# Page loads and fused-pass loads issued by ScalarE, layer-0 fillers by SyncE, in a two-layer GNN and mixture-of-experts kernel

## The chip, the cores and the metric

The kernel runs on one core of one Trainium2 chip. Times are device microseconds (us) of one execution. An execution that the profiler recorded has a span, from the first recorded instruction to the last, and its own time, which is a little longer.

The engines are named as the profile names them: PE (matrix unit; PEld is its weight load), DVE (vector), ACT (scalar), POOL (GpSimd), SP (sync; it has no arithmetic and here only issues DMAs). SPq and ACTq in the profile are instructions of the two engines that only the sequencer executes: DMA issues, register moves, semaphore waits.

## The reference

Two layers over 8192 tokens (128 graphs of 64 nodes) of 256 channels. Each layer is a graph network and then a mixture of experts; both add to the residual.

```python
# layer 0
x = x + gnn0(layernorm(x), adj)          # adj @ x, 256 -> 1024, RMS norm, silu, 1024 -> 256
n = layernorm(x)
logits = einsum('bsd,ed->bse', n, gate_w)                      # 64 experts
top_logits, indices = top_k(logits, 6)
scores = softmax(top_logits)
xW = einsum('bsd,bskde->bske', n, lattice_weights[indices])    # 256 x 256 per expert
lattice_out = einsum('bske,bsk->bse', xW, scores)
proj = einsum('bsd,ed->bse', lattice_out, out_w) + out_b
x = x + layernorm(n + proj) * ln_g + ln_b
# layer 1
n = layernorm(x);  h = layernorm(n) * gamma + beta
x = x + n + relu((adj @ h) @ W_rel + b_rel + h @ W_root)
n = layernorm(x)
x = x + sum over the top 2 of 8 experts of n: w * (relu(n @ W1[e] + b1[e]) @ W2[e] + b2[e])
```

## The kernel before

Four stages follow one another on the core.

**Stage 0, layer 0's graph network (to about 770 us).** It works through 32 blocks of 256 tokens, chooses six experts for each token, and scatters each token's row six times into a table in HBM, `r0x`, so that the rows of one expert lie together (line 277, indirect DMAs of POOL). A row carries its 256 values, the place where its answer belongs, and its weight. A page table is then computed: a page is 128 rows of one expert, and for each page it holds the row where the page starts and the expert.

**Stage 1, the pages of layer 0 (785 to 1476 us).** 447 pages are handled as 224 pairs. Three functions are staggered: at step s the kernel calls `fetch(s + 12)`, `flip(s + 3)` and `apply(s)`.

- `fetch` reads the start rows of four pages from the page table into registers (`Router.load`, line 372, once every second pair) and loads each page of the pair from HBM to a tile `px0` or `px1` (line 378, 129 KB each; 16 buffers of each name).
- `flip` transposes the pair on PE (line 736) into PSUM (`pt`, 4 buffers), and ACT copies it to SBUF (line 738, `pxT`, 5 buffers).
- `apply` multiplies the pair with its experts' matrices on PE (line 751, into `py`, 4 buffers in PSUM), scales each row by its weight on DVE (line 756, `py_s`, 8 buffers), and sends each page's 128 answers to `r0y` in HBM by an indirect DMA of POOL (line 284, `reply`). For the first 64 pairs it also calls `fill_end` (line 361), which stores a page of filler rows behind the rows of one expert in the table (line 157, 129 KB each), so that the last page of an expert that is not full reads defined rows. Full pages come first in the page table and are loaded without waiting for the fillers.

**Stage 2, the fused pass (1476 to 1903 us).** 32 blocks again. For a block, `load3` loads its six answers a token (`y`, 1536 KB, line 793, 2 buffers), the normed input `xn1` and the residual `x1` (lines 795 and 797, 256 KB each, 3 buffers), and two halves of the adjacency (line 473). `mixture` adds the six answers by transposing matmuls (line 807), ACT copies the sum to `accT` (line 810), and `out_proj` multiplies it with `out_w` on PE (line 818). Then come the layer norm, the graph network of layer 1, the choice of two experts and the scatter to `r1x`. The functions are staggered by block: at one step `load3(s + 2)` is called first, `mixture(s + 1)` and `out_proj(s + 1)` after it. `load_w2`, once in each of eight steps, loads one of the eight matrices `fw2` that the last stage needs (512 KB).

**Stage 3, layer 1's experts (1903 to 2449 us).** Pages of 256 rows, their weights loaded by SP, two matmuls, answers added to `out_x` by POOL.

The order of the instructions on PE, DVE and ACT is the one in which the program calls them (`tc.manual_schedule`). The order on SP and POOL is the scheduler's. DMAs of SP and ACT, in the scheduler's order over both, take turns on eight semaphores ("lanes"): each waits until the DMA eight before it has landed.

Before the change SP issues all loads of stages 1 and 2, and ACT issues the fillers:

```python
staggered(npair, ((-12, fetch), (-3, flip), (0, apply)))      # stage 1
staggered(NB, ((-2, load3), (0, layer_out_h), (3, choose1), (-1, mixture), ...))   # stage 2
```

Of the kernel before, what the change touches and what calls it, by code (L numbers as in the profile page):

```python
# [13 lines left out]
ENG = mybir.EngineType  # L14
# [5 lines left out]
P = 128  # L20
# [50 lines left out]
class Router:  # L71
# [286 lines left out]
        v.scalar_tensor_tensor(exp, ispart, -float(E), kind, op0=ALU.mult, op1=ALU.add)  # L358
        v.tensor_scalar(self.tab[:, 1, :], exp, float(E - 1), None, op0=ALU.min)

    def fill_end(self, e):

        if e % 4 == 0:
            _, self.ends = self.nc.values_load_multi_w_load_instructions(
                self.last[0:1, e:e + 4], engines=[ENG.Activation], min_val=0, max_val=self.spare - self.pg,
                skip_runtime_bounds_check_because="the rows of an expert end in its chunk")
        self.fill(self.nc.scalar, self.ends[e % 4])

    def load(self, what, i, engine):

# [3 lines left out]
            skip_runtime_bounds_check_because="the page table holds no other values for any counts")  # L374
        return v

    def fetch(self, i, row, out):
        d = self.nc.sync.dma_start(out=out, in_=self.table[ds(row, self.pg), :].rearrange("(t p) d -> p t d", p=P))  # L378
        if i < self.full_pages:
            self.tc.declare_no_dep(d.ins, group=self.name + "fill", reason="full pages have no filler rows")  # L380
            self.tc.add_to_no_dep_group(self.name + "full", d.ins)
# [11 lines left out]
def two_layer_gnn_moe_kernel(ctx: ExitStack, tc: tile.TileContext, a: dict, out: bass.AP):  # L393
# [8 lines left out]
    C = T * P  # L402
# [57 lines left out]
    def by_tile(ap):  # L460
        return ap.rearrange("(t p) d -> p t d", p=P)
# [5 lines left out]
        nc.gpsimd.memset(at, 0.0)  # L467
        adjacency.append(at)

    def load_adjacency(b):  # L470
        at = adjacency[b % 4]
        for g in range(2):
            nc.sync.dma_start(out=at[g * G:(g + 1) * G, :, g * G:(g + 1) * G],
                              in_=adjT[2 * b * T + g:2 * (b + 1) * T:2].rearrange("t m n -> m t n"))
        return at

# [25 lines left out]
    with tc.tile_pool(name="c0", bufs=1) as c0, \  # L502
# [15 lines left out]
        def load0(b):  # L518
            B = blocks[b]
            B["x"] = x = x_view[:, b % 4 * T:(b % 4 + 1) * T, :]  # L520
            nc.sync.dma_start(out=x, in_=by_tile(x_in[ts(b, C), :]))
            B["at"] = load_adjacency(b)

        load0(0)
        load0(1)
# [187 lines left out]
    with tc.tile_pool(name="wx0", bufs=3) as wx, \  # L713
            tc.tile_pool(name="pt1", bufs=4, space=PSUM) as pt_pool, \
            tc.tile_pool(name="py1", bufs=4, space=PSUM) as py_pool:
        npair = (r0.pages + 1) // 2
        pairs = [dict() for _ in range(npair)]
        regs = {}

        def fetch(j):  # L720
            Q = pairs[j]
            for q in range(2):
                i = 2 * j + q
                if i % 4 == 0:
                    regs["row"] = r0.load(0, i, ENG.SP)
                if i < r0.pages:
                    Q["px", q] = px = wx.tile([P, 1, W], F32, name=f"px{q}", bufs=16)
                    r0.fetch(i, regs["row"][i % 4], px)

        def flip(j):  # L730
            Q = pairs[j]
            pt = pt_pool.tile([P, KD, C], F32, name="pt")
            n = min(2, r0.pages - 2 * j)
            for q in range(n):
                for k in range(KD):
                    nc.tensor.transpose(pt[:, k, ts(q, P)], Q["px", q][:, 0, ts(k, P)], ident)  # L736
            Q["xT"] = xT = wx.tile([P, KD, C], F32, name="pxT", bufs=5)
            nc.scalar.copy(xT[:, :, :n * P], pt[:, :, :n * P])  # L738

        def apply(j):  # L740
            Q = pairs[j]
            if j < E0:
                r0.fill_end(j)
            if j % 2 == 0:
                regs["e"] = r0.load(1, 2 * j, ENG.PE)
            py = py_pool.tile([P, 2, D], F32, name="py")
            y = wx.tile([P, 2, D], F32, name="py_s", bufs=8)
            n = min(2, r0.pages - 2 * j)
            for q in range(n):
                for k in range(KD):  # L750
                    nc.tensor.matmul(py[:, q, :], lhsT=Q["xT"][:, k, ts(q, P)],  # L751
                                     rhs=lat[:, ds(regs["e"][(2 * j + q) % 4], 1), k, :].rearrange("p o d -> p (o d)"),
                                     start=(k == 0), stop=(k == KD - 1))
            for q in range(n):
                px = Q["px", q]
                nc.vector.tensor_scalar(y[:, q, :], py[:, q, :], px[:, 0, D + 1:D + 2], None, op0=ALU.mult)  # L756
                r0.reply(px[:, 0, :], y[:, q, :])

        staggered(npair, ((-12, fetch), (-3, flip), (0, apply)))
    lat_pool.__exit__(None, None, None)  # L760


# [5 lines left out]
    with tc.tile_pool(name="c3", bufs=1) as c3, \  # L768
# [21 lines left out]
        def load3(b):  # L790
            B = blocks[b]
            B["y"] = y = work.tile([P, T, K0, D], F32, name="y")
            nc.sync.dma_start(out=y, in_=r0.answer[ts(b, C * K0), :].rearrange("(t p k) d -> p t k d", p=P, k=K0))
            B["xn1"] = xn1 = work.tile([P, T, D], F32, name="xn1", bufs=3)
            nc.sync.dma_start(out=xn1, in_=by_tile(xn1_dram[b]))
            B["x1"] = x1 = work.tile([P, T, D], F32, name="x1", bufs=3)
            nc.sync.dma_start(out=x1, in_=by_tile(x1_dram[b]))
            B["at"] = load_adjacency(b)

        def mixture(b):  # L800

# [168 lines left out]
    with tc.tile_pool(name="wx1", bufs=2) as wx, \  # L970
            tc.tile_pool(name="pt4", bufs=2, space=PSUM) as pt_pool, \
            tc.tile_pool(name="ph4", bufs=4, space=PSUM) as ph_pool, \
            tc.tile_pool(name="py4", bufs=2, space=PSUM) as py_pool:
        PG = 2 * P
        pages = [dict() for _ in range(r1.pages)]
        regs = {}

        def fetch1(i):
            Q = pages[i]
            if i % 4 == 0:  # L980
                regs["row"], regs["esp"] = r1.load(0, i, ENG.SP), r1.load(1, i, ENG.SP)
            row, e = regs["row"][i % 4], regs["esp"][i % 4]
            Q["x"] = x = wx.tile([P, 2, W], F32, name="px", bufs=4)
            r1.fetch(i, row, x)
            Q["w"] = w = wx.tile([P, F1W], F32, name="pw", bufs=3)
            nc.sync.dma_start(out=w, in_=fw1[ds(e, 1)].rearrange("o p f -> p (o f)"))  # L986
            Q["b2"] = b2 = wx.tile([P, D], F32, name="pb2", bufs=4)
            nc.sync.dma_start(out=b2, in_=a["L1_ffn_b2"][ds(e, 1), :].to_broadcast([P, D]))

        def flip1(i):  # L990
            Q = pages[i]
            pt = pt_pool.tile([P, KD, PG], F32, name="pt")
            ops.transpose(pt, Q["x"])
            Q["xT"] = xT = wx.tile([P, KD, PG], F32, name="pxT")
            nc.scalar.copy(xT, pt)

        def up(i):
            Q = pages[i]
            w = Q["w"]
            Q["hid"] = hid = wx.tile([P, KF, PG], F32, name="phid")  # L1000
            for c in range(KF):
                ph = ph_pool.tile([P, PG], F32, name="ph")
                for k in range(KD):
                    nc.tensor.matmul(ph, lhsT=w[:, k * F1 + c * P:k * F1 + (c + 1) * P], rhs=Q["xT"][:, k, :],  # L1004
                                     start=(k == 0), stop=(k == KD - 1))
                nc.scalar.activation(hid[:, c, :], ph, AF.Relu, bias=w[:, KD * F1 + c:KD * F1 + c + 1], scale=1.0)  # L1006

        def down(i):
            Q = pages[i]
            if i < E1:  # L1010
                r1.fill_end(i)
            if i % 4 == 0:
                regs["e"] = r1.load(1, i, ENG.PE)

            p = wx.tile([P, 2], F32, name="p")
            nc.scalar.activation(p, Q["x"][:, :, D + 1], AF.Exp)  # L1016
            nc.vector.tensor_scalar(p, p, 1.0, None, op0=ALU.add)  # L1017
            nc.vector.reciprocal(p, p)
            py = py_pool.tile([P, 2, D], F32, name="py")
            y = wx.tile([P, 2, D], F32, name="py_s")  # L1020
            for t in range(2):
                for c in range(KF):
                    nc.tensor.matmul(py[:, t, :], lhsT=Q["hid"][:, c, ts(t, P)],  # L1023
                                     rhs=fw2[:, ds(regs["e"][i % 4], 1), c, :].rearrange("p o d -> p (o d)"),
                                     start=(c == 0), stop=(c == KF - 1))
            nc.vector.tensor_add(y, py, Q["b2"].unsqueeze(1).to_broadcast([P, 2, D]))  # L1026
            for t in range(2):
                nc.vector.tensor_scalar(y[:, t, :], y[:, t, :], p[:, t:t + 1], None, op0=ALU.mult)
                r1.add(i, Q["x"][:, t, :], y[:, t, :])

        staggered(r1.pages, ((-2, fetch1), (0, flip1), (1, down), (0, up)))
# [32 lines left out]
```

## Time and profile before

| | |
|---|---|
| median of 14 runs | 2449.61 us (2442.52 to 2479.59) |
| profiled execution: its own time | 2451.15 us |
| profiled execution: its span | 2449.1 us |
| PE busy, share of the span | 2072.6 us, 85% |
| PEld | 1758.9 us, 72% |
| DVE | 1238.9 us, 51% |
| ACT | 1047.5 us, 43% |
| POOL | 1249.6 us, 51% |

The span in 40 equal slices of 61 us; each digit is the busy share of a slice in tenths, PEclk the granted clock of PE:

```
PE   3998888888862888888788877899997799999997
DVE  3778888888864222222222324788876222222221
ACT  2877767777751111211111113566554233333332
POOL 1165666666566666666666660333333344444344
PEclk9999999999985899989999999998998899999999
DMA  7133333333364777655555437878772676666665
```

Stage 0 is slices 1 to 13, stage 1 slices 13 to 24, stage 2 slices 25 to 31, stage 3 the rest. In the rows of the profile, L378 is line 378 of the kernel; a row of a group has the line, the engine, the operation, the tiles written and read, the count, the busy time and the mean of one in ns, the idle time of the engine ahead of them, and what ended most of that. In the table of waits a row names who waited for whom, the total in us, the times, and the longest.

HBM traffic over the span is 404 MB, 167 GB/s on average. SP issued 447 loads of px in stage 1 and 32 loads of each kind (64 adjacency halves) in stage 2; ACT issued the 64 fillers.

### The profile page before, as it was taken

How to read it: one execution, taken by the hardware profiler on the slowest of the kernel's cores; microseconds unless marked ns; L12 is line 12 of the kernel's file. 1: busy time of each engine (PE TensorE's matmuls, PEld its weight loads, DVE VectorE, ACT ScalarE, POOL GpSimd, SP SyncE). 2: the span in 40 equal slices, each digit the busy share in tenths (PEclk: the TensorE clock that was granted, in tenths of full speed). 3: DMA queues.
4: the chain of work that ended last, by engine and by line, in shares of the span. 5: the costliest groups of instructions: out<-in, count | busy, mean ns of one | idle time of the engine just before them, and what ended most of it. 6: DMA issues, size and time to landing. Idle time of an engine off the chain costs nothing. (4 is left out here: it accounts for less than half of the span.)

```text
span 2449.1 us, 38858 instructions
## 1 busy us (share of the span) xinstructions
PE 2072.6 (85%) x10870; PEld 1758.9 (72%) x10870; DVE 1238.9 (51%) x4053; ACT 1047.5 (43%) x2061; POOL 1249.6 (51%) x1238
## 2 busy tenths in 40 slices
PE   3998888888862888888788877899997799999997
PEld 3877777777751776766666666788776688888886
DVE  3778888888864222222222324788876222222221
ACT  2877767777751111211111113566554233333332
POOL 1165666666566666666666660333333344444344
PEclk9999999999985899989999998999998899999999
DMA  7133333333364777655555437878772676666665
GB/s 222 57 123 108 112 120 114 108 115 113 111 206 132 223 223 216 191 161 171 167 175 162 138 100 272 266 250 266 242 236 79 171 170 163 167 158 162 155 163 116
DMA packets 289696, 404.39 MB, mean 165 GB/s; under 512 B 57657, under 2 KB 243273, under 8 KB 289489
## 3 DMA queue, kind: packets, MB, share of 16 engines
q1 hardware_dynamic: 205168, 251.04, 34.4%
q0 software_dynamic: 66480, 136.68, 18.5%
q10 hardware_dynamic: 17840, 14.21, 1.8%
q8 instruction: 94, 1.54, 0.3%
q14 instruction: 114, 0.93, 0.1%
HBM read 228.78 MB, written 181.23 MB: 167 GB/s over the span
## 5 line engine op out<-in xcount | busy, mean ns | idle before, releaser
L284 POOL DMA_INDIRECT r0y<-py_s,px x447 | 439.1, 982 | 251.3 <-DVE py_s L756 127.2
L751 PE MATMUL py<-lat,pxT 128*128 x1788 | 470.6, 405 | 67.9 <-issue 52.4
L277 POOL DMA_INDIRECT r0x<-xs,r0row x384 | 411.2, 1071 | 202.7 <-issue 101.1
L756 DVE TENSOR_SCALAR py_s<-py,px 128x256 f32<-128x256 f32 x447 | 186.9, 478 | 506.7 <-PE py L751 181.3
L751 PEld LDWEIGHTS py<-lat,pxT 128*128 128x128 f32 x1788 | 343.4, 203 | 128.2 <-issue 70.4
L292 POOL DMA_INDIRECT out_x<-py_s,px x142 | 221.1, 1557 | 319.2 <-DMA out_x<-py_s,px 209.3
L738 ACT COPY pxT<-pt 128x512 f32<-128x512 f32 x224 | 125.7, 588 | 582.8 <-remote 173.2
L1006 ACT ACTIVATE phid<-ph,pw 128x256 f32<-128x256 f32 x284 | 134.7, 474 | 334.3 <-issue 210.7
L1004 PE MATMUL ph<-pxT,pw 128*128 128x256 f32 x1136 | 258.8, 381 | 2.4 <-DMA pw<-in_L_ffn_W1b 2.4
L1023 PE MATMUL py<-fw,phid 128*128 x1136 | 256.9, 379 | 0.0
L618 PE MATMUL ps<-lat 128*128 128x256 f32 x1024 | 254.0, 392 | 0.7 <-issue 0.7
L1004 PEld LDWEIGHTS ph<-pxT,pw 128*128 128x128 f32 x1136 | 217.2, 191 | 32.7 <-issue 2.8
L575 PE MATMUL ph<-lat 128*128 128x256 f32 x1024 | 232.7, 386 | 3.3 <-DVE lat L609 1.4
L1023 PEld LDWEIGHTS py<-fw,phid 128*128 128x128 f32 x1136 | 210.4, 190 | 25.7
L736 PE MATMUL pt<-ident,px 128*128 128x128 f32 x894 | 153.9, 290 | 83.0 <-DMA px<-r0x 69.9
L277 POOL DMA_INDIRECT r1x<-xs,r1row x128 | 127.7, 998 | 178.5 <-issue 83.9
L575 PEld LDWEIGHTS ph<-lat 128*128 128x128 f32 x1024 | 195.1, 193 | 30.5 <-DVE lat L609 2.1
L618 PEld LDWEIGHTS ps<-lat 128*128 128x128 f32 x1024 | 192.6, 195 | 26.2 <-issue 2.7
L736 PEld LDWEIGHTS pt<-ident,px 128*128 128x128 f32 x894 | 118.4, 150 | 126.5 <-issue 64.6
L578 ACT ACTIVATE lat<-ph,c_L_gnn_b 128x256 f32<-128x256 f32 x256 | 102.1, 469 | 112.0 <-PE ph L575 85.6
L1017 DVE TENSOR_SCALAR p<-p 128x2 f32<-128x2 f32 x71 | 13.6, 191 | 249.8 <-ACT p L1016 239.7
L1026 DVE TENSOR_TENSOR py_s<-py,pb 128x512 f32<-128x512 f32 x71 | 49.1, 692 | 159.0 <-PE py L1023 156.8
(259 smaller groups left out, 3004.2 us busy)
## 6 DMA issues: line engine op xcount, KB each, us to landing
px<-r0x SPq DMA_DIRECT2D x447, 129.0 KB
y<-r0y SPq DMA_DIRECT2D x32, 1536.0 KB
pw<-in_L_ffn_W1b SPq DMA_DIRECT2D x71, 514.0 KB
px<-r1x SPq DMA_DIRECT2D x71, 258.0 KB
x<-x SPq DMA_DIRECT2D x64, 256.0 KB
pb<-in_L_ffn_b SPq DMA_DIRECT2D x71, 128.0 KB
r0x<-r0filler ACTq DMA_DIRECT2D x64, 129.0 KB
lat<-in_x SPq DMA_DIRECT2D x32, 256.0 KB
```

The costliest lines, as they stand in the source:

```text
L277: i = self.nc.gpsimd.indirect_dma_start(out=self.table[:, :], out_offset=bass.IndirectOffsetOnAxis(ap=row[:, t, k:k + 1], axis=0), in_=xs[ ...
L284: i = self.nc.gpsimd.indirect_dma_start(out=self.answer[:, :], out_offset=bass.IndirectOffsetOnAxis(ap=x[:, self.D:self.D + 1].bitcast(I32 ...
L292: i, d = f"{self.name}add{i}", self.nc.gpsimd.indirect_dma_start(out=self.total[:, :], out_offset=bass.IndirectOffsetOnAxis(ap=x[:, self.D ...
L575: nc.tensor.matmul(ph[:, c, :], lhsT=w1[:, k, ts(2 * j + c, P)], rhs=B["aggT"][:, k, :], start=(k == 0), stop=(k == KD - 1))
L618: nc.tensor.matmul(B["po"][:, t, :], lhsT=B["hT"][:, c, ts(t, P)], rhs=w2[:, c, :], start=(c == 0), stop=(c == KH - 1))
L736: nc.tensor.transpose(pt[:, k, ts(q, P)], Q["px", q][:, 0, ts(k, P)], ident)
L738: nc.scalar.copy(xT[:, :, :n * P], pt[:, :, :n * P])
L751: nc.tensor.matmul(py[:, q, :], lhsT=Q["xT"][:, k, ts(q, P)], rhs=lat[:, ds(regs["e"][(2 * j + q) % 4], 1), k, :].rearrange("p o d -> p (o ...
L756: nc.vector.tensor_scalar(y[:, q, :], py[:, q, :], px[:, 0, D + 1:D + 2], None, op0=ALU.mult)
L1004: nc.tensor.matmul(ph, lhsT=w[:, k * F1 + c * P:k * F1 + (c + 1) * P], rhs=Q["xT"][:, k, :], start=(k == 0), stop=(k == KD - 1))
L1006: nc.scalar.activation(hid[:, c, :], ph, AF.Relu, bias=w[:, KD * F1 + c:KD * F1 + c + 1], scale=1.0)
L1023: nc.tensor.matmul(py[:, t, :], lhsT=Q["hid"][:, c, ts(t, P)], rhs=fw2[:, ds(regs["e"][i % 4], 1), c, :].rearrange("p o d -> p (o d)"), st ...
```

## The change

The issuing engine of three groups of DMAs changes; what is loaded and stored, the buffers and the staggering stay.

- `fetch` of the first 12 pairs (24 pages) is still issued by SP. From pair 12 on, the two loads of a pair and the register loads that they need are issued by ACT, and stand in ACT's order where the program calls them: ahead of the copy of the pair nine before.
- The 64 fillers of layer 0, with their register loads, are issued by SP. The fillers of layer 1 are still ACT's.
- The loads of the fused pass (`y`, `xn1`, `x1` and the adjacency, five DMAs a block) are issued by ACT, ahead of the copy of `accT` in the same step. Stage 0 loads its adjacency by SP as before.
- The loads of stage 3 stay with SP.

With this SP's own order changes as well: 16 of the fillers come ahead of the first page, then the first 24 pages, then the other 48 fillers; after them SP has the `fw2` loads, which are no longer behind block loads, and the stores of the fused pass. The eight `fw2` loads stand together at the start of the fused pass, two ahead of the store of filler rows into `r1x` and six after it.

```diff
-    def fill_end(self, e):
+    def fill_end(self, e, engine, eng):
 
         if e % 4 == 0:
             _, self.ends = self.nc.values_load_multi_w_load_instructions(
-                self.last[0:1, e:e + 4], engines=[ENG.Activation], min_val=0, max_val=self.spare - self.pg,
+                self.last[0:1, e:e + 4], engines=[eng], min_val=0, max_val=self.spare - self.pg,
                 skip_runtime_bounds_check_because="the rows of an expert end in its chunk")
-        self.fill(self.nc.scalar, self.ends[e % 4])
+        self.fill(engine, self.ends[e % 4])
...
-    def fetch(self, i, row, out):
-        d = self.nc.sync.dma_start(out=out, in_=self.table[ds(row, self.pg), :].rearrange("(t p) d -> p t d", p=P))
+    def fetch(self, i, row, out, engine):
+        d = engine.dma_start(out=out, in_=self.table[ds(row, self.pg), :].rearrange("(t p) d -> p t d", p=P))
...
-    def load_adjacency(b):
+    def load_adjacency(b, engine):
         at = adjacency[b % 4]
         for g in range(2):
-            nc.sync.dma_start(out=at[g * G:(g + 1) * G, :, g * G:(g + 1) * G],
+            engine.dma_start(out=at[g * G:(g + 1) * G, :, g * G:(g + 1) * G],
...
-            B["at"] = load_adjacency(b)
+            B["at"] = load_adjacency(b, nc.sync)
...
+        AHEAD = 12
...
         def fetch(j):
             Q = pairs[j]
+            first = j < AHEAD
             for q in range(2):
                 i = 2 * j + q
                 if i % 4 == 0:
-                    regs["row"] = r0.load(0, i, ENG.SP)
+                    regs["row"] = r0.load(0, i, ENG.SP if first else ENG.Activation)
                 if i < r0.pages:
                     Q["px", q] = px = wx.tile([P, 1, W], F32, name=f"px{q}", bufs=16)
-                    r0.fetch(i, regs["row"][i % 4], px)
+                    r0.fetch(i, regs["row"][i % 4], px, nc.sync if first else nc.scalar)
...
             if j < E0:
-                r0.fill_end(j)
+                r0.fill_end(j, nc.sync, ENG.SP)
...
-        staggered(npair, ((-12, fetch), (-3, flip), (0, apply)))
+        staggered(npair, ((-AHEAD, fetch), (-3, flip), (0, apply)))
...
         def load3(b):
             B = blocks[b]
             B["y"] = y = work.tile([P, T, K0, D], F32, name="y")
-            nc.sync.dma_start(out=y, in_=r0.answer[ts(b, C * K0), :].rearrange("(t p k) d -> p t k d", p=P, k=K0))
+            nc.scalar.dma_start(out=y, in_=r0.answer[ts(b, C * K0), :].rearrange("(t p k) d -> p t k d", p=P, k=K0))
             B["xn1"] = xn1 = work.tile([P, T, D], F32, name="xn1", bufs=3)
-            nc.sync.dma_start(out=xn1, in_=by_tile(xn1_dram[b]))
+            nc.scalar.dma_start(out=xn1, in_=by_tile(xn1_dram[b]))
             B["x1"] = x1 = work.tile([P, T, D], F32, name="x1", bufs=3)
-            nc.sync.dma_start(out=x1, in_=by_tile(x1_dram[b]))
-            B["at"] = load_adjacency(b)
+            nc.scalar.dma_start(out=x1, in_=by_tile(x1_dram[b]))
+            B["at"] = load_adjacency(b, nc.scalar)
...
-            r1.fetch(i, row, x)
+            r1.fetch(i, row, x, nc.sync)
...
-                r1.fill_end(i)
+                r1.fill_end(i, nc.scalar, ENG.Activation)
```

## The prediction

> **What bounds the kernel now.** I read the mean over long windows first, then the rows of the groups, the table of waits, and last the timeline of a few microseconds. Three of the four stages are touched: the pages of layer 0 (785 to 1476 us), the fused pass (1476 to 1903), and the seam between them. The last stage (1903 to 2449) keeps its own loads and its own fillers.
>
> POOL over the page stage, columns: window, length, POOL busy (instructions), granted clock, DMA share, GB/s.
>
> ```profile
> 805.00:1052.00 247.00, 157.57 (x161) 0.91 0.68 207
> 1052.00:1457.00 405.00, 262.81 (x268) 0.94 0.51 155
> ```
>
> 161 replies in 247 us are 1.534 us each, 268 in 405 us are 1.511. A reply costs POOL 0.98 us and follows the last at 1.29 us when it can, as the timeline shows; so POOL has a floor of 447 x 1.288 = 576 us here and runs 676 (first reply at 796.2, last at 1472.6). The rest is gaps:
>
> ```profile
> L284 POOL DMA_INDIRECT r0y<-py_s,px x447 | 439.1, 982 | 251.3 <-DVE py_s L756 127.2
> ...
> 1105.48 0.98 POOL L284 DMA_INDIRECT r0y<-py_s,px  x1 [0.30 <-issue]
> 1108.94 0.98 POOL L284 DMA_INDIRECT r0y<-py_s,px  x1 [2.49 <-DVE py_s L756]
> ...
> 1096.24 0.59 ACT L738 COPY pxT<-pt 128x512 f32<-128x512 f32 x1 [1.43 <-PE pt L736]
> 1107.44 0.59 ACT L738 COPY pxT<-pt 128x512 f32<-128x512 f32 x1 [10.61 <-remote]
> ```
>
> The stage goes in cycles: 10 replies in a row and a gap of 2.2 us more than the step (15.1 us), or 8 and 1.9 (12.2 us). While POOL runs, PE's semaphore updates arrive late (up to 9 us behind the end of the matmul), ACT sits before its copy, and both come through once POOL is dry. POOL's chain, not the copies, sets the stage.
>
> Now the loads. The table of waits and two stretches of SP's timeline:
>
> ```profile
> ACT pxT L738 <- DMA px<-r0x: 76.0, 17, 10.5
> PE pt L736 <- DMA px<-r0x: 69.9, 27, 37.3
> PEld pt L736 <- DMA px<-r0x: 41.6, 32, 2.6
> PE po L818 <- ACT accT L810: 19.6, 14, 2.5
> ...
> 1103.78 2.86 SPq L378 DMA_DIRECT2D px<-r0x  x2
> ...
> 1108.08 1.59 SPq L378 DMA_DIRECT2D px<-r0x  x3
> ```
>
> Inside this run of replies SP's two loads start 2.85 us apart (2.2 in the run's first half); in the gap, three start at 1108.08, 1108.74 and 1109.46, 0.69 apart. The lead of a pair's second load over its first flip is 14 to 17 us for pairs 16 to 110 and 2.3 us from pair 144 on: there SP has become as slow as its consumers, which are the 74 us of PE waits (69.9 + 41.6 less the first 37.3). ACT does not step so:
>
> ```profile
> L378 SPq MOVE px<-r0x x447: 2/29/716, 785.0 to 1453.5; - x149
> ...
> L157 ACTq MOVE r0x<-r0filler x64: 29/29/29, 792.7 to 986.2; - x64
> L157 ACTq DMA_DIRECT2D r0x<-r0filler x64: 338/338/2103, 792.8 to 994.8; - x64
> ```
>
> (minimum/median/maximum ns). 47 of ACT's 64 fillers were issued well inside runs of replies; three took above 600 ns.
>
> The fused pass is PE's:
>
> ```profile
> 1600.00:1700.00 100.00, 98.65 (x646) 86.39 (x645) 87.19 (x385) 61.43 (x130) 36.12 (x42) 1.00 0.80 259
> ...
> 1656.62 1.08 ACT L862 ACTIVATE s<-x,bn_nm,bn_rs 128x256 f32<-128x256 f32 x2
> 1656.69 2.82 PE L807 MATMUL ps<-ident,y 128*128 128x128 f32 x24
> 1659.61 0.59 ACT L810 COPY accT<-ps 128x512 f32<-128x512 f32 x1 [1.90 <-PE ps L807]
> 1660.24 1.13 PE L818 MATMUL po<-m_L_ffn_out_wT,accT 128*128 128x256 f32 x4
> ```
>
> (the first line: PE, PEld, DVE, ACT, POOL). ACT has room on average, but L818 starts as accT ends: that copy is on PE's path, and ACT's free time lies right ahead of it.
>
> **The change, part by part.**
>
> *423 page loads and their register loads from SP to ACT.* ACT issues while its last copy still runs (a filler's register load began 13 ns after a copy), so a pair costs it two issues of some 0.5 us (29 + 37 + 338 ns and the steps between), each second pair 0.31 more: about 1.2 us, 1.9 with a copy that nothing covers, against 3.0 us a pair. Behind them in ACT's order stands the copy of the pair nine earlier; PE's L751 and so DVE and POOL wait for that. A load waits for the release of its px buffer, the reply of the pair seven before that copy, landed 2.3 us after issue. I replayed it on the times of before: each copy at the earliest 1.32 us after the one ahead, and 2.3 + 1.32 us after that reply. Copies move by 1.3 us on average, 5.5 at most, and none passes the start of its own L751. So I price the order at 0. The loads gain: a lead of 9 pairs, 27 us. But where the lead was already 14 us the cycles were the same 15.1 us; with 2.3 us they are a mixture of 15.1/10 and 12.2/8, on average 1.515 us a reply. All tens would be 1.510: 190 x 0.005 = -1 us. The bounds are wide: 100 us for POOL at its floor below, and above what ACT would cost if it stepped as SP does (rival 3).
>
> A rule speaks against a gain: the Trainium skill, "DMA: Bandwidth & Descriptors", section "Issuing engines are not separate DMA queues", says that issuing from several engines saves only the sequencer's time, usually small beside the DMA. Here SP's 2.2 to 2.85 us a page are as long as a landing, 2.3, so the row disagrees on "small"; by the rule the part is 0, by the 74 us of waits taken whole, -74. POOL's unchanged cycles decide for nearly 0.
>
> *64 layer-0 fillers from ACT to SP.* In 37 places an ACT filler stood over 0.5 us for its lane (HW DMAs of both engines take turns on eight; each waits for the landing of the one eight before), 136 us together, the 76 us of ACT's waits above among them, with copies behind. Their stretch is the slower one: 161 x (1.534 - 1.511) = -4 us, bounds -4 and 0. On SP, 16 fillers go ahead of the first page: SP idles there till 784.7 for the last sends; without that cover 16 x 0.4 = 6 us. The other 48 follow page 24, one a pair, and a page's lane is then 8 DMAs, 2.7 pairs, old: landed. Cost 0.
>
> *160 loads of the fused pass to ACT.* SP's issues take (medians) 0.42, 0.36, 0.36, 0.607, 0.607 us: 2.35, with some 0.07 between, 2.7 us. They stand after the second L862 (start 1657.11) and before accT, which would start at 1657.13 + 2.7 + 0.06 = 1659.89, not 1659.61: +0.28 us. About 16 of 31 blocks are that tight (2.49 us from one to the other); in the rest accT already comes 0.4 to 2.3 us later and covers it. 16 x 0.28 = +5 us; bounds 0 and 31 x 0.6 = +18, were every block tight and the issues 0.3 us slower. A load of y now leaves 10.8 us ahead of its use and lands after 6 to 9: hidden; the margin is 2 us.
>
> *The seam.* SP, free of loads, issues the eight 512-KB fw2 loads in a row, two and then six, instead of one a block. From 1457 to 1476 DMA is 38% busy, but y of block 0 moves from 1476 at over 400 GB/s. +1 us; bounds -1 and six of them, 3 MB, ahead of y at 421 GB/s, +7.
>
> Sum: -1 - 4 + 5 + 1 = +1 us on the profiled execution's 2451.2 (span 2449.1), 2452. The median of the 14 runs, 2449.6, is 1.5 lower: 2451.
>
> **Rivals.**
>
> 1. (forecast) Two small things cancel: 2451, its own range 2440 to 2464. Chance 0.45.
>
> 2. SP's steps and PE's late semaphores have one cause, and with SP's page loads gone, PE's updates come through. For it: both are slow in the same runs. Against: the updates were latest (2.0 us on average from 1100 to 1200) when SP mostly waited, and 1.0 where it stepped all the time. Halving the gaps of 57 cycles (102 us) gives -51: 2451 - 51 + 5 = 2405. Chance 0.25.
>
> 3. (slower) ACT takes over SP's steps, its copies behind them. With c us of ACT a pair inside a run and 1.6 in the 2.2-us gap, a cycle makes n = 2.576n/c + 1.4 pairs; at five pairs nothing is lost, which holds until c = 3.6 us. SP's stepping would give up to 5. At c = 4.2, n = 3.6, the cycle is 11.4 us, 3.19 us a pair instead of 3.02: 212 x 0.17 = +36: 2487. Against: ACT's fillers. Chance 0.20.
>
> 4. (slower) The fused pass takes its upper price, +18, and the seam +5: 2451 + 13 + 4 = 2468. Chance 0.10.
>
> **How the numbers follow.** This kernel's measurement tells 0.2%, 5 us, from no change. Case 1 splits 0.10 faster, 0.20 same, 0.15 slower; with 2, 3 and 4: 0.35, 0.20, 0.45. The range goes from case 2's middle to just over case 3's, 2404 to 2490, and leaves about 0.2 outside.
>
> **What would show it.** Page stage: SP silent after the fillers; no PE wait for px; POOL's cycles still 8 to 10 replies. If runs get longer, rival 2; if 4 to 7 and ACT's MOVE rows reach 700 ns, rival 3. Fused pass: accT 0.3 us after the mixture's end, PE near 96%. A direct wait of L807 for y after block 0 would make the margin of 2 us wrong.

## The result and the profile after

| | before | after |
|---|---|---|
| median | 2455.41 us (47 runs, 2437.89 to 2479.59) | 2481.72 us (10 runs, 2477.19 to 2489.94) |
| ratio, 95% interval | | 1.0116 [1.0088, 1.0143] |
| profiled execution, own time | 2451.15 us | 2475.38 us |
| its span | 2449.1 us | 2473.2 us |

The change costs 26 us by these medians, 28 by the ratio and 24 between the two profiled executions; it was to cost nothing that can be measured. The two profiled executions, stage by stage (times of starts in the two traces):

| stretch | before | after | difference |
|---|---|---|---|
| to the first reply of layer 0 | 796.2 | 797.4 | +1.2 |
| first to last reply (the page stage) | 676.4 | 677.5 | +1.1 |
| last reply to accT of block 2 (the seam) | 30.6 | 41.7 | +11.1 |
| accT of block 2 to accT of block 31 | 353.1 | 363.4 | +10.3 |
| from there to the end | 592.9 | 593.3 | +0.4 |

The page stage takes as long as it did. POOL in the same two windows of the profile after (window, length, POOL busy, granted clock, DMA share, GB/s):

```profile
805.00:1052.00 247.00, 157.88 (x161) 0.93 0.65 200
1052.00:1457.00 405.00, 262.52 (x269) 0.91 0.51 155
```

161 and 269 replies, before 161 and 268. The lead of a pair's loads over its flip is now 19 to 24 us (medians of 16 pairs, from pair 16 on) and no longer 2.3 at the end of the stage; PE's wait for px after the start is gone; POOL's 57 gaps, 101.9 us together beyond the usual step between replies, have become 53 of 103.4. What SP did inside runs of replies ACT now does, though less often. The rows of line 378 after, on ACT (minimum/median/maximum ns):

```profile
L378 ACTq FUSED_REGOPS  x423: 3/37/709, 792.6 to 1432.1; - x141
L378 ACTq MOVE px<-r0x x423: 2/29/711, 792.7 to 1432.2; - x141
```

In the page stage, 30 of the 423 MOVEs take over 600 ns; of SP's 447 before, 73 did.

The first loss is the seam. Three engines' timelines after, from the last reply on (ACT, SP, PE; the time in brackets is idle time of the engine and what ended it):

```profile
1478.00 0.45 ACTq L795 DMA_DIRECT2D y<-r0y  x1
...
1479.61 12.62 ACTq L473 DMA_DIRECT2D at<-in_adjT  x2
1494.38 0.38 ACTq L795 DMA_DIRECT2D y<-r0y  x1
1495.95 0.37 ACTq L797 DMA_DIRECT2D xn<-xn  x1
...
1497.59 1.28 ACTq L473 DMA_DIRECT2D at<-in_adjT  x2
1498.96 0.59 ACT L812 COPY accT<-ps 128x512 f32<-128x512 f32 x1 [36.77 <-issue]
...
1478.08 12.19 SPq L942 DMA_DIRECT2D fw<-in_L_ffn_W  x6
...
1487.70 4.55 PE L809 MATMUL ps<-ident,y 128*128 128x128 f32 x24 [21.23 <-DMA y<-r0y]
...
1499.60 3.78 PE L820 MATMUL po<-m_L_ffn_out_wT,accT 128*128 128x256 f32 x8 [7.13 <-ACT accT L812]
```

PE ends block 0's mixture at 1492.25 and stands 7 us for accT. ACT isn't busy: it has issued the first half of block 0's adjacency at 1479.61 and the second only at 1491.63, and behind that stand block 1's five loads, and then accT. The semaphore records of the trace tell what these loads stand for: the lane of the second half was held by an fw2 load of SP (issued 1480.28, landed 1491.61), and three of block 1's loads stand for lanes of fw2 loads once more (landed 1494.36, 1495.93 and 1497.57). Before, the waits of these loads were SP's, and ACT's copy followed the mixture at once:

```profile
1489.62 0.59 ACT L810 COPY accT<-ps 128x512 f32<-128x512 f32 x1 [31.77 <-PE ps L807]
...
1490.26 1.99 PE L818 MATMUL po<-m_L_ffn_out_wT,accT 128*128 128x256 f32 x8 [0.30 <-ACT accT L810]
```

Of the 11.1 us, 6.6 are this stand. Another 2.6 are matmuls that run slower behind it: L820 takes 3.78 us and not 1.99, the next mixture 3.65 and not 2.78; the granted clock is 0.74 from 1488 to 1517, before 0.84 from 1484 to 1503. 1.4 are a later accT of block 2, and 0.4 are y: block 0's mixture ends 17.4 us after the last reply, before 16.9.

The second loss is in the length of the blocks, which comes in two kinds in both traces: 11.29 us, with accT 0.09 us behind the mixture's end, and mostly 12.6 to 13.3 us, with accT mostly 1.4 to 2 us behind it. From block 3 on, before has 14 blocks over 12.4 us and after has 24. One of the long ones after (timelines of POOL, PE and ACT):

```profile
1710.20 1.04 POOL L277 DMA_INDIRECT r1x<-xs,r1row  x1 [2.03 <-DVE bn_rs L857]
...
1714.09 0.96 POOL L277 DMA_INDIRECT r1x<-xs,r1row  x1 [0.31 <-issue]
...
1711.72 2.82 PE L809 MATMUL ps<-ident,y 128*128 128x128 f32 x24
...
1716.61 0.70 PE L820 MATMUL po<-m_L_ffn_out_wT,accT 128*128 128x256 f32 x2 [1.32 <-ACT accT L812]
...
1715.97 0.59 ACT L812 COPY accT<-ps 128x512 f32<-128x512 f32 x1 [3.24 <-PE pos L181]
```

ACT's loads of this step are out by 1713.14, ahead of the mixture's end at 1714.54, so they are not what accT waits for. In the long blocks POOL's four sends run while the mixture runs; in a block of 11.29 us (the one that the prediction shows) they start 0.2 us ahead of its end, and 0.2 to 1.8 us ahead in blocks 11 to 21 of before.

One thing has to be known to read the experiments: in every one of their sessions the kernel before took 2299 to 2304 us and not 2450 to 2455. No trace of the kernel before was kept from these sessions; f1_fills and e2_fused, whose page loads are SP's too, stand for it. In them PE's semaphore updates are not late (in the page stage the median is 0.01 us behind the instruction's end, against 1.9 in the profile before), SP does not step, nor does ACT in b_after, POOL's replies run without gaps, and nearly all blocks take 11.29 us. Each ratio is against the kernel before in the same session.

### The profile page after: what moved, and what is told of

It is laid out like the page before. It is cut to its first block, busy times and chain, and to the rows that moved or that the text cites. A ratio compares the mean times of both kernels' runs of the same rounds, so it can differ in the third digit from the quotient of the medians.

```text
span 2473.2 us, 38568 instructions
## 1 busy us (share of the span) xinstructions
PE 2082.8 (84%) x10870; PEld 1766.2 (71%) x10870; DVE 1238.7 (50%) x4053; ACT 1052.3 (43%) x2061; POOL 1251.1 (51%) x1238
## 5 line engine op out<-in xcount | busy, mean ns | idle before, releaser
L753 PE MATMUL py<-lat,pxT 128*128 x1788 | 482.4, 408 | 78.1 <-issue 71.9
L753 PEld LDWEIGHTS py<-lat,pxT 128*128 128x128 f32 x1788 | 347.2, 205 | 139.5 <-issue 92.0
L740 ACT COPY pxT<-pt 128x512 f32<-128x512 f32 x224 | 130.8, 585 | 581.1 <-remote 207.0
L1006 PEld LDWEIGHTS ph<-pxT,pw 128*128 128x128 f32 x1136 | 216.9, 191 | 32.4 <-issue 2.7
```

## The experiments

All twelve. The kernels of one session ran on one chip. The profiled executions by stage, in us; the second column says who issues the page loads and, for ACT, how many pairs ahead of `apply`:

| kernel | page loads | first to last reply (gaps) | last reply to accT of block 2 | accT 2 to accT 31 | ratio to before [95%] |
|---|---|---|---|---|---|
| f1_fills | SP | 573.6 (0) | 29.7 | 328.9 | 1.0001 [0.9990, 1.0012] |
| e1_pages | ACT, 12 | 582.3 (7) | 29.9 | 327.9 | 1.0041 [1.0027, 1.0055] |
| e2_fused | SP | 573.6 (0) | 37.9 | 328.8 | 1.0053 [1.0033, 1.0073] |
| b_after | ACT, 12 | 579.1 (6) | 39.1 | 328.7 | 1.0075 [1.0061, 1.0089] |
| e3_seam | ACT, 12 | 582.7 (10) | 31.5 | 328.8 | 1.0053 [1.0033, 1.0072] |
| e4_w2 | ACT, 12 | 579.4 (7) | 30.4 | 332.4 | 1.0058 [1.0043, 1.0072] |
| e7_ahead8 | ACT, 8 | 575.4 (2) | 39.2 | 329.0 | 1.0051 [1.0038, 1.0064] |
| c1_fix | ACT, 8 | 576.4 (2) | 32.4 | 331.3 | 1.0024 [1.0014, 1.0034] |
| e5_hold_before | SP | 573.8 (0) | 29.9 | 327.5 | 1.0010 [0.9998, 1.0022] |
| h1_hold | SP | 573.6 (0) | 28.9 | 326.0 | 1.0025 [1.0015, 1.0035] |
| h2_hold | SP | 573.9 (0) | 28.8 | 326.0 | 1.0029 [1.0017, 1.0040] |
| e8_hold_after | ACT, 12 | 581.2 (9) | 38.1 | 327.7 | 1.0085 [1.0072, 1.0099] |

Sessions: e1, e2, e3, e5; then b, e4, e7, h1; then c1, f1, e8; then h2.

### One part of the change at a time

e1_pages is the change with the fused pass's loads given back to SP (the edit as against the changed kernel, as in e3 and e4 below):

```diff
-            nc.scalar.dma_start(out=y, in_=r0.answer...
+            nc.sync.dma_start(out=y, in_=r0.answer...
-            B["at"] = load_adjacency(b, nc.scalar)
+            B["at"] = load_adjacency(b, nc.sync)
```

(xn1 and x1 likewise.)

> Only the page stage is changed (423 page loads on ScalarE, fillers on SyncE); the fused pass's loads are SyncE's again. Theory A (the whole loss is in the fused pass: about 13 us at its start and the rest in blocks that fall into a slower phase of 12.6 us): ratio to before 1.000, between 0.996 and 1.004; first to last reply 676 us, within 6; fused-pass blocks as in before, a mixture of 11.3 and 12.6 us. Theory B (the page stage loses too, in executions other than the profiled one): ratio 1.004 or more.

Measured 1.0041, so close to the bound of both theories that the ratio doesn't separate them. The trace does: the replies take 582.3 us where f1_fills takes 573.6, 9 us more, all of it as gaps between 800 and 850 us. Theory A falls, the page stage does lose. Why it lost only 1.1 us in the first profile after, where the replies have gaps anyway, this run doesn't show.

e2_fused is the other half: `fetch` all on SP, `fill_end(j, nc.scalar, ENG.Activation)`, and the fused pass's loads on ACT.

> Only the fused pass's 160 loads are ScalarE's; the page stage is as in before. Theory A: the whole loss, ratio 1.009 to 1.014, first accT about 9 us and first send to r1x about 14 us later after the last reply than in before, and most blocks at 12.6 us. Theory B: clearly less than the whole change, under 1.008.

Measured 1.0053, 12.5 us: less than theory A said and within theory B's bound, while the place is A's. AccT of block 2 comes 8 us later after the last reply than in e1, and the blocks after it are of the same length: 328.8 and 327.9 us for 29 of them. Five loads a block on ACT cost nothing there. Some 4 us of the 12.5 are in no stage that the edit touches.

b_after is the change itself in such a session.

> The changed kernel itself, beside the kernel before and the other three on the same chip. If this chip runs POOL's replies without gaps in the kernel before (as the first four experiments' chip did), the parts add: 9 us in the page stage (e1_pages) and 10 to 13 in the fused pass (e2_fused), ratio 1.008 to 1.011. If it shows the gaps of 2 us, as the first profiles did: page stage 0, 13 us at the start of the fused pass, and the rest from blocks in the slow phase, ratio 1.009 to 1.014.

Measured 1.0075, 17 us, just under the range and 4.6 us under the sum of the two parts (9.1 + 12.5 in medians). So of the 26 to 28 us of the first measurement about 17 are left where the late updates are absent.

f1_fills moves the fillers alone (the edit as against the kernel before):

```diff
-                r0.fill_end(j)
+                r0.fill_end(j, nc.sync, ENG.SP)
```

> Only the 64 fillers go to SyncE; all loads stay with SyncE. Theory D (the page stage loses by copies behind loads on ScalarE): ratio 0.998 to 1.002, no gap in the replies where before has none. Theory E (the fillers on SyncE are what holds the pages, through the shared lanes): 6 to 9 us, ratio 1.003 to 1.004, with gaps in the first 70 us.

1.0001 and no gap in the replies: the fillers on SP cost nothing as long as SP issues the page loads too. That speaks against theory E only so far: with the page loads on ACT, the fillers' lanes do hold them, as the next part shows.

### What holds the pages

The first 70 us of the page stage by POOL's busy time (window, length, POOL, clock, DMA share, GB/s), for f1_fills:

```profile
780.00:850.00 70.00, 53.35 (x55) 1.00 0.86 258
```

for b_after:

```profile
780.00:850.00 70.00, 48.53 (x50) 1.00 0.98 295
```

50 replies and not 55. The first reply of b_after comes at 781.0, so that 54 would fit; four are lost, 5 us. Inside the window, SP's timeline and then ACT's and POOL's, of b_after:

```profile
784.26 48.56 SPq L157 DMA_DIRECT2D r0x<-r0filler  x48
...
818.13 2.52 ACTq L378 DMA_DIRECT2D px<-r0x  x2
820.75 0.59 ACT L740 COPY pxT<-pt 128x512 f32<-128x512 f32 x1 [2.26 <-DMA r0y<-py_s,px]
...
821.34 0.98 POOL L284 DMA_INDIRECT r0y<-py_s,px  x1 [1.31 <-DVE py_s L758]
```

The two loads take 2.52 us and not 0.9, since the second stands; the copy follows both, and POOL runs dry. What the second stands for is not what the row of the copy names. A load waits for two semaphores, its lane and the reply that frees its px buffer. By the trace's records that reply had landed at 811.03; the lane was held by a filler of SP, issued at 815.45 and landed at 820.16, and the load went out at 820.32. So it is all over this window: while SP has its 48 fillers to issue, 20 page loads of ACT stand for more than 0.3 us, 23 us together, and each of them goes on when its lane lands, 12 times a filler and 8 times a page load. SP issues three fillers to a pair there, so that a lane eight DMAs old is often only 4 to 6 us old and not landed. Once the fillers are out, page loads do stand for their px buffers, over 200 times and some 200 us in all, and after 848 us POOL has no gap.

In the table of waits of this trace PE waits 53.0 us and PEld 77.0 for ACT's copy ahead of L753, in f1_fills 2.8 and 10.7. The two overlap, and they are no price: e7_ahead8 below still has 46.8 and 66.4.

e7_ahead8 gives a load more room between its buffer's release and its use, `AHEAD = 8`.

> The changed kernel with AHEAD = 8: page loads stand eight pairs ahead of apply and not twelve, so a load waits for the reply of the pair sixteen before it, which is now eleven and not seven pairs before the copy behind it in ScalarE's order. Theory D (in the first 70 us of the page stage ScalarE's copies stand behind loads whose px buffer has not been released): on a chip without POOL gaps in before the 9 us go, 7 to 10 us less than b_after; with POOL's gaps, within 3 us of it. Theory E (the fillers' lanes hold the loads): no difference beyond 3 us either way.

The replies take 575.4 us with two gaps, the median is 4.7 us under b_after's, and the same window, in the columns above, holds 54 replies of at most 55:

```profile
780.00:850.00 70.00, 52.07 (x54) 1.00 0.97 296
```

DMA is as full as in b_after (0.97 and 0.98), so a full DMA alone doesn't hold the replies. The direction and the place are theory D's; the size expected was too large, as the change's own page stage beside it lost 5.5 us and not 9. But D's reason, the px buffer, is not what the traces show: here too the loads of the window stand for lanes, 12 times and 16 us instead of 20 and 23. Why they stand less with `AHEAD = 8` isn't shown, and no run has page loads on ACT with no fillers in the lanes.

### What holds the seam

e3_seam lets SP issue the loads of blocks 0 and 1:

```diff
+            q = nc.sync if b < 2 else nc.scalar
-            nc.scalar.dma_start(out=y, ...
+            q.dma_start(out=y, ...
```

> The changed kernel, but the loads of the first two blocks of the fused pass are SyncE's, ahead of its fw2 loads; blocks 2 to 31 stay ScalarE's. Theory A: the 13 us at the start go, ratio 1.004 to 1.008 instead of 1.0116; accT of block 0 within 0.2 us of its mixture's end; later blocks still mostly at 12.6 us. Theory C (the loss is the five issues ahead of accT in every block, 0.3 us each): 1.010 or more, and the blocks 0.3 us longer than before's in either phase.

AccT of block 0 follows its mixture by 0.1 us, and accT of block 2 comes 31.5 us after the last reply: the seam is back to within 2 us of e1_pages'. The ratio, 1.0053, lies in theory A's range. The blocks afterwards are nearly all at 11.29 us, not at 12.6 as theory A thought; theory C's 0.3 us a block is in no trace.

e4_w2 leaves all block loads on ACT and takes SP's fw2 loads out of the way:

```diff
-                nc.sync.dma_start(out=fw2[:, e], ...
+                nc.scalar.dma_start(out=fw2[:, e], ...
```

> The changed kernel, with the eight fw2 loads issued by ScalarE at the end of steps 4 to 11 instead of by SyncE at the start of the fused pass. Theory A1 (ScalarE's second adjacency load at the start stands for the lane of an fw2 load, with block 1's loads and accT behind it): accT of block 0 within 0.3 us of its mixture's end instead of 6.7, 8 to 13 us less than b_after. Theory A2 (the five loads in front of accT cost that by their issue time alone, whatever the lanes): within 3 us of b_after.

The seam in b_after (ACT, and SP's fw2 loads):

```profile
1363.77 12.19 ACTq L473 DMA_DIRECT2D at<-in_adjT  x2
...
1363.41 11.13 SPq L942 DMA_DIRECT2D fw<-in_L_ffn_W  x6
...
1381.26 0.59 ACT L812 COPY accT<-ps 128x512 f32<-128x512 f32 x1 [44.27 <-DMA fw<-in_L_ffn_W]
```

and in e4_w2:

```profile
1363.42 1.35 ACTq L473 DMA_DIRECT2D at<-in_adjT  x2
1364.80 0.61 ACTq L795 DMA_DIRECT2D y<-r0y  x1
...
1372.84 0.58 ACT L812 COPY accT<-ps 128x512 f32<-128x512 f32 x1 [38.61 <-PE ps L809]
```

Same loads, same engine, same order; without the fw2 loads in the lanes the two halves of the adjacency go out in 1.35 us and accT waits for PE alone. Theory A1 is shown for the place. In time it brought 2.7 us and not 8 to 13. The seam gained 8.7 us (30.4 and not 39.1), and the fw2 loads, now among ACT's instructions of steps 4 to 11, make blocks there longer (332.4 us and not 328.7 for the 29 blocks). That leaves 5 us; the medians' 2.7 are not accounted for further.

c1_fix repairs both places, `AHEAD = 8` and SP for the loads of blocks 0 and 1.

> The changed kernel with both repairs: AHEAD = 8, and the loads of the fused pass's first two blocks by SyncE. If the two parts are the whole loss where all blocks take 11.29 us, ratio 0.999 to 1.003 (e7_ahead8 and e3_seam add: the page stage within 2 us of 573.6, accT of block 2 30 to 32 us after the last reply). If something else is lost too: 1.004 or more. Where blocks fall into the slow phase of 12.6 us: 1.002 to 1.008.

The ratio, 1.0024, is within the range: 5.7 us of 17 are left. The stages just miss what was expected of them: 576.4 us of replies and not 575.6 at most, accT of block 2 at 32.4 us and not 32. Against f1_fills the trace shows 2.8 us in the replies, 2.7 in the seam and 2.4 in the blocks behind it; its execution is c1_fix's slowest, 11 us above the median, so these needn't add up to the 5.7. No version here is faster than the kernel before.

### The long blocks

The kernel with the cast of POOL's row numbers one step later; it ran three times on the kernel before (e5, h1, h2) and once on the change (e8):

```diff
-            r1.send(r1.places(b, B["hot"]), B["xs"])
+            B["rowf"] = r1.places(b, B["hot"], cast=False)
+        def send1(b):
+            B = blocks[b]
+            r1.send(r1.cast(B["rowf"]), B["xs"])
...
             (3, choose1),
+            (4, send1),
             (-1, mixture),
```

> The kernel before with one DVE instruction moved: the cast of the row numbers that POOL's sends to r1x wait for comes in the next step, after choose1, so that a block's four sends start at the end of the next block's mixture and not some 4 us before it. Theory A (PE's semaphore updates are held while the sends run; sends that start early delay accT by 1.4 us, and the early phase keeps itself going): all blocks from the fourth on at 11.3 us, ratio 0.986 to 0.994, and runs that differ less from one another. Theory C (the phase has nothing to do with the sends): ratio 0.998 to 1.004, and still a mixture of 11.3 and 12.6 us.

> Once more the kernel before with the cast of POOL's row numbers one step later, on another chip if it is one. Where before's fused-pass blocks are a mixture of 11.3 and 12.6 us (PE's semaphore updates come late while POOL sends): all of them at 11.3, ratio 0.986 to 0.996. Where they are all at 11.3 already: 1.000 to 1.002, as measured.

> The changed kernel with the cast of POOL's row numbers one step later, so that no send to r1x runs ahead of a mixture's end. On a chip with late semaphore updates: blocks 5 to 31 at 11.3 us instead of 12.6, which is 10 to 30 us less in the fused pass, ratio 0.998 to 1.008 instead of 1.0116. On a chip without: 1.007 to 1.011, as b_after within 4 us.

> The kernel before with the cast of POOL's row numbers one step later, a third time, for the chance of a chip on which before takes some 2450 us. There, if sends ahead of a mixture's end are what makes blocks of 12.6 us: all blocks from the fifth on at 11.3 us, ratio 0.986 to 0.996; if they are not: a mixture as before, 0.998 to 1.004. On a chip on which before takes some 2300 us: 1.000 to 1.003, which tells nothing new.

None of the four settles it. There were no long blocks to shorten in these sessions, so the edit only cost its own 3 to 7 us, and e8 is the change within its error. Whether sends that run ahead of the mixture's end make the long blocks is argued from two traces and not shown. By themselves they don't: in b_after, from block 5 on, all but one block's start 2 to 3.8 us ahead of it, and accT still follows the mixture by 0.09 us (0.16 once); it would take the late updates as well. Open as well is whether the change brings them on: before, too, goes from blocks of 11.29 to long ones at block 22 in its trace and scatters over 42 us in 47 runs, while the ten runs after lie within 13.

## Why the prediction was right and wrong

The time, 2481.7, lies in the range of 2404 to 2490, on the side that had 0.45. The likeliest case, two small things that cancel, was wrong, and so was its own range of 2440 to 2464. That the wide range holds is luck: its upper end came from ACT stepping as SP does, whose price didn't come, and the time was lost in the seam, priced at +1, and in the length of the blocks, which had no price.

- *POOL's cycles, not the loads, set the page stage.* Right in the profile after: loads 20 us early changed the replies by 1.1 us. The rule of the Trainium skill that was weighed, "Issuing engines are not separate DMA queues" in "DMA: Bandwidth & Descriptors", gave 0 for this part and was nearer than the 74 us of waits. (Those 74 also add two engines that stand idle at the same time; together PE and PEld stood 41 us.)
- *The order on ACT, priced at 0.* Right in the total for that execution, wrong where POOL has no gaps: 5.5 to 9.1 us in five traces. The replay let a load wait for its px buffer, and for that wait the 0 stands. What it left out is the lane. The prediction took it as landed: "The other 48 follow page 24, one a pair". They come three to a pair, and ACT's loads stood 23 us for lanes in b_after. In the profile after, too, ACT stood 27 us ahead of 19 page loads while the fillers went out; the first 100 us of replies there hold 64 and not 66, and later runs of replies made that up. That the pauses in that trace are the cover is argued and not shown.
- *The fillers, -4.* No gain: the stretch from 805 to 1052 us holds 161 replies after as before, and f1_fills is 1.0001.
- *The issues ahead of accT, +5.* Nothing, 11.29 us a block with and without them. The estimate let the first issue begin with the second L862; it begins 1.36 us earlier. ACT's and PE's timelines of b_after:

```profile
1577.11 0.60 ACT L860 ACTIVATE hn<-x,bn_nm,bn_rs 128x256 f32<-128x256 f32 x1
1577.24 0.37 ACTq L795 DMA_DIRECT2D y<-r0y  x1
...
1578.60 0.59 ACT L864 ACTIVATE s<-x,bn_nm,bn_rs 128x256 f32<-128x256 f32 x1
1578.75 1.32 ACTq L473 DMA_DIRECT2D at<-in_adjT  x2
...
1581.09 0.59 ACT L812 COPY accT<-ps 128x512 f32<-128x512 f32 x1 [1.90 <-PE ps L809]
...
1578.18 2.82 PE L809 MATMUL ps<-ident,y 128*128 128x128 f32 x24
```

The loads stand behind four activations in the order and are issued while the first of them runs; the last is out at 1580.07, 0.9 us ahead of the mixture's end.

- *The seam, +1, bounds -1 and +7.* The step that failed: 11.1 us in the profile after, 8 to 9.5 in the experiments. The prediction priced the bytes of fw2 beside y, and these cost 0.4. What happened is a wait: a lane held by an fw2 load, the adjacency load standing for it on ACT, and behind that block 1's loads and accT. What is queued behind a waiting instruction was asked for the page stage, and there of the px buffer alone, and not here.
- *The blocks' length.* The prediction saw that accT comes 0.4 to 2.3 us late in half of the blocks and used it as cover; that the number of such blocks could change, 10.3 us in the two profiles, was in no term. Why it changed stays open.
- *Rival 2* (PE's updates come through once SP is idle) fell: PE's updates are as late after as before (medians 1.8 and 1.9 us in the page stage), and the gaps as long. *Rival 3* (ACT takes over the stepping) happened in kind, 30 MOVEs over 600 ns, and not in price: most of POOL's runs still hold ten replies. *Rival 4*, 2468, had the place right, the fused pass and the seam, with the price on the wrong one of the two.

## What to carry to other kernels

A load on an engine that computes is not priced by its issue time: in the steady state that was free, and what the experiments could place of the loss came from the semaphore waits that the load brings into the engine's order, with a copy behind them. Both times the wait was for a lane, held for the most part by another engine's DMA. So for each load that is moved ask what it waits for, a buffer's release or a lane shared with another queue, what else holds that lane once the old queue runs free, and whose work stands behind it. And a replay on an old trace takes that trace's pauses as given, and knows only the waits that it is told of; price the term once more without the pauses, and with every semaphore that the load waits for.

## What the runs showed of the hardware

The same kernel took 2450 to 2455 us in one set of sessions and 2299 to 2304 in another. In the first, while POOL's indirect DMAs run back to back, PE's semaphore updates come up to 9 us late and the sequencer that issues page loads takes some 0.7 us for single steps, SP before and ACT after. In the second, neither is there. The granted clock of an execution is 0.94 in the first and 0.96 in the second. The traces differ in one more thing: the two of the first set hold 22,076 and 24,142 recorded semaphore updates, that of f1_fills 43,255, so that how late an update is, in the first set, is read from the records that are there. The row of e2_fused, where SP issues all page loads as before:

```profile
L378 SPq MOVE px<-r0x x447: 29/29/38, 766.6 to 1313.3; - x149
```

38 ns at most, before 716. What sets this is open; with it POOL's page stage is 103 us shorter (573.6 and 676.4 us).
